# Moving the difference of the split fields from GpSimd to VectorE for ten fields, and loading fields five ahead

## Chip, cores, metric

One core of one Trainium2 chip. The metric is the device time of one execution in microseconds (us), lower is better. The kernel before took 770.79 us in the three runs that came with it (769.37 to 772.43).

## The reference, cut

```python
# inputs: (1024, 32, 128) fp32; W: (496, 128, 128) fp32, one matrix for each pair i < j of the 32 fields
v_i = inputs[:, I_IDX, :]
v_j = inputs[:, J_IDX, :]
transformed = jnp.einsum('bpd,ped->bpe', v_i, W)
return transformed * v_j          # (1024, 496, 128) fp32, 260 MB
```

## The kernel before

Pairs are taken row by row: first the row of field 30 (one pair), then that of 29 (two pairs), down to field 0 (31 pairs). The first 15 pairs use fp32 matmuls as they are ("native"). From pair 15 on, each operand is split into a high part `h`, a low part `l` and a difference `d`, and three faster matmuls take the place of the native one. Splitting a weight chunk (two pairs) is one ScalarE and three GpSimd instructions, splitting a half of a field likewise:

```python
    def split_x(f, a):
        ...
        nc.scalar.mul(h, x_sb[f][:, s], 1.0 - 2.0**-13)
        nc.gpsimd.tensor_tensor(l, x_sb[f][:, s], h.bitcast(F32), ALU.subtract)
        nc.gpsimd.tensor_scalar(l, l.bitcast(F32), 1.0 / EPS, 1.0, ALU.mult, ALU.mult)
        nc.gpsimd.tensor_tensor(d, h.bitcast(F32), l.bitcast(F32), ALU.subtract)
```

A unit is half a pair (512 of 1024 columns). VectorE multiplies each unit's result in PSUM by field j into an output tile of two pairs, of which there are four; a full tile (1 MB) is stored.

```python
    for u in range(2 * NQ + LAG):
        q = u // 2
        if u % (2 * WL) == 0 and (q // WL + WLEAD) * WL < NQ:
            load_w(q // WL + WLEAD)                  # four pairs of weights, 2 KB a partition
        if u < 2 * NQ:
            i, j = pairs[q]
            if u % 2 == 0 and j == i + 1 and 0 <= i - 2 - XLEAD:
                load_x(i - 2 - XLEAD)                # one field, 4 KB a partition
            first(u)                                 # two matmuls, ScalarE scales the sum
        if u >= LAG:
            second(u - LAG)                          # third matmul, VectorE product, store
        ...                                          # every second unit: one split, if any is due
```

All loads but four, and all stores, are issued in order from one queue (SP).

## Time and profile before

| | before |
|---|---|
| time | 770.79 us |
| bytes moved | 310.11 MB: 260.05 MB of results written, 49.28 MB of inputs read, the rest mostly instructions |
| busy: PE, VectorE, ScalarE, GpSimd | 715, 625, 634, 612 us of 769 |
| stretches of 3 us with a DMA share under 0.96, between 3 and 270 us | 6.0 us in sum |

The page's DMA row gives the mean busy share of the 16 DMA engines; in the views of stretches a row has the stretch, its length, the busy time of each engine (with the number of instructions), the granted clock, the DMA share and GB/s. The share can read a little over 1.00 in a full stretch. A stretch whose share is clearly under 1 is called a hole below.

### The profile page before, as it was taken

To read this page: it belongs to the slowest core of one execution; us is meant where nothing else is said; L and a number is where in the kernel's file an instruction comes from. 1 tells how busy PE (TensorE), PEld (TensorE's weight loads), DVE (VectorE), ACT (ScalarE), POOL (GpSimd) and SP (SyncE) were. 2 spreads that over 40 slices of the span, in tenths; PEclk is the share of its full clock that TensorE was granted. 3 is DMA by queue.
4 is the path that set the end of the run, shared out by engine and by line. 5 is a ranking of instruction groups with operands and counts; after the bars stand their busy time and mean duration, and the time that the engine had idled before them with its cause. 6 is when DMAs were issued, how large, how long until landed. Compare 5 with 4: busy or idle time off the path is not lost.

```text
span 769.2 us, 11797 instructions
## 1 busy us (share of the span) xinstructions
PE 715.0 (93%) x2946; PEld 548.9 (71%) x2946; DVE 625.3 (81%) x992; ACT 633.9 (82%) x1256; POOL 611.6 (80%) x883
## 2 busy tenths in 40 slices
PE   7989879889999898999998999999999999999994
PEld 3566657778777686776776877777777777777773
DVE  4767788888988787887787988888888888888885
ACT  2278878888888898898888989898889898998983
POOL 1988998998989878778778697878787869697660
PEclk9999999999999999999999999999999999999997
DMA  9899998999999999999999999999999999999997
GB/s 357 369 411 420 421 400 345 417 410 380 414 422 405 403 395 421 395 416 411 401 420 415 406 414 418 419 415 418 402 419 409 410 410 407 411 413 402 401 399 307
DMA packets 59108, 310.11 MB, mean 403 GB/s; under 512 B 6560, under 2 KB 6816, under 8 KB 27424
## 3 DMA queue, kind: packets, MB, share of 16 engines
q1 hardware_dynamic: 58464, 308.31, 98.8%
q10 hardware_dynamic: 576, 1.05, 0.4%
q8 instruction: 24, 0.39, 0.2%
q14 instruction: 44, 0.36, 0.1%
HBM read 49.28 MB, written 260.05 MB: 402 GB/s over the span
## 4 chain that ended last, share of the span: by engine, by line
PE 49%; DMA 32%; DVE 11%; POOL 6%; issue 1%; DVEq 0%; SPq 0%; ACT 0%; POOLq 0%
DMA out_dram<-ot 31%; PE po L151 31%; PE po L160 15%; DVE ot L166 11%; PE po L148 4%; POOL xd L109 2%; POOL wl L93 1%; POOL xl L107 1%; POOL wd L95 1%; POOL xl L108 0%; DMA x<-in_xt_dram 0%; POOL wd L94 0%; DVEq L166 0%; SPq L74 0%; ACT xh L106 0%
## 5 line engine op out<-in xcount | busy, mean ns | idle before, releaser
L166 DVE TENSOR_TENSOR ot<-po,x 128x512 f32<-128x512 f32 x992 | 625.3, 685 | 135.5 <-DMA out_dram<-ot 71.9
L152 ACT ACTIVATE po<-po 128x512 f32<-128x512 f32 x962 | 549.7, 583 | 109.7 <-PE po L151 61.4
L151 PE MATMUL po<-xh,wh 128*128 128x512 f32 x962 | 387.0, 402 | 25.0 <-DVE ot L166 23.9
L151 PE MATMUL po<-xl,wl 128*128 128x512 f32 x962 | 380.0, 395 | 14.6 <-POOL wl L93 14.1
L160 PE MATMUL po<-xd,wd 128*128 128x512 f32 x962 | 377.3, 393 | 0.0
L151 PEld LDWEIGHTS po<-xh,wh 128*128 128x128 f32 x962 | 181.5, 189 | 96.8 <-DVE ot L166 58.4
L93 POOL TENSOR_TENSOR wl<-w,wh 128x256 fp32r<-128x256 f32 x241 | 177.8, 738 | 74.2 <-ACT wh L92 74.2
L151 PEld LDWEIGHTS po<-xl,wl 128*128 128x128 f32 x962 | 181.9, 189 | 53.9 <-POOL wl L93 19.7
L160 PEld LDWEIGHTS po<-xd,wd 128*128 128x128 f32 x962 | 182.0, 189 | 39.0 <-ACT po L152 0.4
L95 POOL TENSOR_TENSOR wd<-wl,wd 128x256 fp32r<-128x256 f32 x241 | 177.8, 738 | 20.1
L94 POOL TENSOR_SCALAR wd<-wh 128x256 fp32r<-128x256 f32 x241 | 97.4, 404 | 20.3
L92 ACT ACTIVATE wh<-w 128x256 fp32r<-128x256 f32 x241 | 99.0, 412 | 0.0
L107 POOL TENSOR_TENSOR xl<-x,xh 128x512 fp32r<-128x512 f32 x52 | 67.2, 1292 | 17.0 <-ACT xh L106 17.0
L109 POOL TENSOR_TENSOR xd<-xh,xl 128x512 fp32r<-128x512 f32 x52 | 67.0, 1288 | 4.3
L106 ACT ACTIVATE xh<-x 128x512 fp32r<-128x512 f32 x52 | 32.5, 629 | 11.9 <-DMA x<-in_xt_dram 11.7
L108 POOL TENSOR_SCALAR xl<-xl 128x512 fp32r<-128x512 f32 x52 | 32.2, 620 | 4.6
L148 PE MATMUL po<-x,w 128*128 128x512 f32 x60 | 28.9, 647 | 3.9 <-DMA x<-in_xt_dram 3.9
L148 PEld LDWEIGHTS po<-x,w 128*128 128x128 f32 x60 | 12.3, 207 | 19.7 <-issue 15.1
L106 ACT ACT_TABLE_LOAD x1 | 1.3, 1283 | 2.6 <-issue 2.6
L203 POOL MEMSET const-float32-0.0<- 128x1 f32 x1 | 0.1, 98 | 0.2 <-issue 0.2
L203 POOL MEMSET const-bfloat16-1.0<- 128x1 bf16 x1 | 0.1, 101 | 0.0
L203 POOL MEMSET const-uint8-127<- 128x1 uint8 x1 | 0.1, 101 | 0.0
(1 smaller groups left out, 0.1 us busy)
## 6 DMA issues: line engine op xcount, KB each, us to landing
out_dram<-ot SPq DMA_DIRECT2D x247, 1024.0 KB, 8.9
w<-in_wt_dram SPq DMA_DIRECT2D x123, 256.0 KB, 9.1
x<-in_xt_dram SPq DMA_DIRECT2D x30, 512.0 KB, 9.2
x<-in_xt_dram ACTq DMA_DIRECT2D x4, 256.0 KB, 4.9
out_dram<-ot SPq DMA_DIRECT2D x4, 256.0 KB, 7.0
w<-in_wt_dram SPq DMA_DIRECT2D x1, 192.0 KB, 3.5
w<-in_wt_dram SPq DMA_DIRECT2D x1, 64.0 KB, 2.9
```

Source lines behind the costliest of these rows:

```text
L92: nc.scalar.mul(h, raw, 1.0 - 2.0**-13)
L93: nc.gpsimd.tensor_tensor(l, raw, h.bitcast(F32), ALU.subtract)
L94: nc.gpsimd.tensor_scalar(d, h.bitcast(F32), EPS, 1.0, ALU.mult, ALU.mult)
L95: nc.gpsimd.tensor_tensor(d, l.bitcast(F32), d.bitcast(F32), ALU.subtract)
L106: nc.scalar.mul(h, x_sb[f][:, s], 1.0 - 2.0**-13)
L107: nc.gpsimd.tensor_tensor(l, x_sb[f][:, s], h.bitcast(F32), ALU.subtract)
L109: nc.gpsimd.tensor_tensor(d, h.bitcast(F32), l.bitcast(F32), ALU.subtract)
L148: nc.tensor.matmul(po[u], w_raw[q // WL][:, q % WL, :], x_sb[i][:, s], start=True, stop=True)
L151: nc.tensor.matmul(po[u], w_s[c][t][:, r], x_s[i][t][:, s], start=t == 0, stop=t == 1)
L152: nc.scalar.mul(po[u], po[u], 1.0 + EPS)
L160: nc.tensor.matmul(po[u], w_s[q // WC][2][:, r], x_s[i][2][:, s], start=False, stop=True, skip_group_check=True)
L166: nc.vector.tensor_tensor(ots[g][:, k, s], po.pop(u), x_sb[j][:, s], ALU.mult)
```

## The change

The intent: GpSimd, which the early rows wait for, gives up the difference of the ten fields split first (25 to 16), and VectorE forms it, at most ten units after the split was issued; fields are fetched five rows ahead instead of three.

```diff
+SHARED = 10
+XDLAG = 10
-XLEAD = 3
+XLEAD = 5
...
     def split_x(f, a, u):
...
-        nc.gpsimd.tensor_tensor(d, h.bitcast(F32), l.bitcast(F32), ALU.subtract)
+        if f > NF - 2 - NATIVE - SHARED:
+            later.append((min(u + XDLAG, 2 * first_q[f] + LAG - 1), d, h.bitcast(F32), l.bitcast(F32)))
+        else:
+            nc.gpsimd.tensor_tensor(d, h.bitcast(F32), l.bitcast(F32), ALU.subtract)
...
+        while later and later[0][0] <= u:
+            nc.vector.tensor_tensor(*later.pop(0)[1:], ALU.subtract)
```

More of the change, by code (lines that the diff above doesn't have):

```diff
@@ L85, with split_w @@
     w_s = {}
-    def split_w(c):
+    def split_w(c, u):
         k = c * WC % WL
@@ L98, with split_x @@
     x_s = {}
-    def split_x(f, a):
+    later = []
+    def split_x(f, a, u):
         if a == 0:
@@ L118 @@
     for c in range(c0, nchunk):
-        todo.append(((c - 3) * WC + 1, max(c * WC, nq0), lambda c=c: split_w(c)))
+        todo.append(((c - 3) * WC + 1, max(c * WC, nq0), lambda u, c=c: split_w(c, u)))
     for i in range(NF - 2 - NATIVE, -1, -1):
         for a in range(0, BT, HB):
-            todo.append((first_q[i + 1] + 1 if i < NF - 3 - NATIVE else 2, first_q[i], lambda i=i, a=a: split_x(i, a)))
+            todo.append((first_q[i + 1] + 1 if i < NF - 3 - NATIVE else 2, first_q[i], lambda u, i=i, a=a: split_x(i, a, u)))
     todo.sort(key=lambda t: t[1])
@@ L185 @@
             if ready:
-                ready[0][2]()
+                ready[0][2](u)
                 todo.remove(ready[0])
-    assert not todo
+        while later and later[0][0] <= u:
+            nc.vector.tensor_tensor(*later.pop(0)[1:], ALU.subtract)
+    assert not todo and not later
 def kernel(**inputs):
```

## The prediction

> **What bounds the kernel now.** I read the page first (part 1 and the DMA lines), then the busy time by stretches, cut ever finer, then the waits, then the DMA queue's own waits in the first 60 us, last the order of instructions on each engine. The page:
>
> ```profile
> span 769.2 us, 11797 instructions
> PE 715.0 (93%) x2946; PEld 548.9 (71%) x2946; DVE 625.3 (81%) x992; ACT 633.9 (82%) x1256; POOL 611.6 (80%) x883
> DMA  9899998999999999999999999999999999999997
> DMA packets 59108, 310.11 MB, mean 403 GB/s; under 512 B 6560, under 2 KB 6816, under 8 KB 27424
> ```
>
> No compute engine is full, but the DMA row is 9 nearly everywhere: 310.11 MB have to move, the same bytes before and after. So I look for the places where the DMA was not full. Busy time by stretches (columns: PE, PEld, VectorE, ScalarE, GpSimd, then granted clock, DMA share, GB/s):
>
> ```profile
> 3.00:33.00 30.00, 29.09 (x62) 12.77 (x63) 20.02 (x30) 4.12 (x8) 15.63 (x18) 1.00 1.03 416
> 33.00:36.00 3.00, 3.00 (x15) 2.45 (x14) 1.61 (x3) 2.65 (x6) 2.83 (x5) 1.00 0.15 59
> 36.00:114.00 78.00, 68.39 (x279) 52.09 (x277) 59.47 (x94) 63.12 (x128) 70.70 (x96) 0.98 1.01 413
> 117.00:120.00 3.00, 3.00 (x10) 2.36 (x10) 1.94 (x3) 1.41 (x4) 2.75 (x5) 0.66 0.48 191
> 120.00:123.00 3.00, 3.00 (x15) 2.49 (x14) 3.00 (x6) 2.80 (x6) 2.69 (x5) 1.00 0.77 279
> 177.00:180.00 3.00, 3.00 (x14) 2.48 (x13) 2.59 (x5) 2.43 (x5) 2.44 (x4) 0.99 0.77 314
> 180.00:744.00 564.00, 540.90 (x2291) 422.45 (x2290) 473.71 (x762) 498.78 (x987) 456.30 (x669) 1.00 1.01 410
> ```
>
> From 180 to 744 us the DMA share is 1.01 at 410 GB/s: that stretch is DMA-bound and nothing in the change touches its bytes. The holes are early: 33:36 loses 0.85 x 3 = 2.55 us, 117:123 loses 1.56 + 0.69 = 2.25 us, 177:180 loses 0.69 us, together **5.5 us**. A further half microsecond goes at 267:270 (share 0.82), past the changed fields. The start (share 0.32 in the first 3 us: 2 us) and the end (last pairs without loads, last stores landing, about 5 us) stay.
>
> What made the holes? The waits of the whole run, and the DMA queue's waits in 0:60:
>
> ```profile
> POOL wl L93 <- ACT wh L92: 74.2, 99, 2.0
> DVE ot L166 <- DMA out_dram<-ot: 71.9, 84, 3.3
> PEld po L151 <- POOL wl L93: 19.7, 14, 2.7
> PE po L151 <- POOL wl L93: 14.1, 13, 2.3
> ```
>
> ```profile
> SPq L83 <- POOL wl L93: 8.8, 1, 8.8
> ```
>
> VectorE waits 71.9 us for stores to free an output tile: the DMA bound again. PE waits for GpSimd's `wl` 14.1 us; cut by stretches nearly all of it lies before 200 us: 3.1 us in 38:115, 2.3 us (one wait) in 115:135, 5.2 us in 135:173. The wait at 115.7 us stands right before the hole at 117, and in the order of instructions GpSimd there does an x split (1.30 + 0.62 + 1.26 us) ahead of that `wl`. The 8.8 us wait of the DMA queue is one weight load, held until 34.2 us, when GpSimd's third `wl` ends; the stores stand behind it in the same queue, the previous store was issued at 25.0, and the DMA ran dry at 33. So the early holes all carry GpSimd's name.
>
> **What the skill says.** "VectorE: DVE Perf Modes", section on the TRN2 errata, gives (N+151)/0.96 ns for an fp32 `tensor_tensor`, 691 ns at N = 512. The trace has 685 ns for VectorE's 128x512 product and, back to back, 2.50 us for 4, so 0.625 us each: agreed. "SBUF — State Buffer", section "Who interferes with whom", says that a VectorE instruction with two SBUF inputs contends with a GpSimd instruction that reads SBUF, and that whichever comes second fully blocks. Before has no such VectorE instruction (its first input is in PSUM), so this trace can't show it; it does show GpSimd's 128x512 subtraction at 1.27 us at 16 us and 1.30 at 111 us beside a busy VectorE, so today's products don't disturb it. "HBM Reference", section "Specifications (TRN2)", has about 425 GB/s for a core streaming alone; the trace's 410 to 416 over long stretches is close under that, so a faster DMA isn't to be hoped for.
>
> **The change, part by part.** Fields 25 to 16 (ten, two halves each) lose GpSimd's `xd` subtraction: 20 x 1.29 (row L109, 1288 ns) = 25.8 us off GpSimd. VectorE gains 20 x about 0.65 = 13 us, and if the lock holds each also waits up to one GpSimd instruction (0.4 to 1.3 us, mean maybe 0.5), so 13 to 23 us; and GpSimd is stopped 20 x 0.65 = 13 us. Net relief of GpSimd: 13 to 26 us, all before about 200 us.
>
> Against the DMA, row by row. A row with n pairs moves n x (0.524 MB out + 0.066 MB weights) and one field of 0.524 MB, at 413 GB/s: 1.43 n + 1.27 us. GpSimd before, by its cadence (a weight chunk of two pairs starts every 1.98 us, a half field every 3.28 us): 0.99 n + 6.56. First row after the native ones, n = 6: GpSimd 12.5 against DMA 9.9; equal at n = 12. Summed over n = 6 to 12, GpSimd lacks 9.3 us, of which the fields fetched ahead cover a part: that fits 5.5 us of holes. After: two halves cost 2 x 1.99 = 4.0, with the lock 5.3 us; GpSimd then needs 0.99 n + 5.3, at n = 6 11.2 against 9.9, and lacks 2.9 us in all with the lock, 0 without. VectorE after, at n = 6: 12 x 0.625 + 2 x 1.1 = 9.7 against 9.9; at n = 10 14.7 against 15.6. Tight, but under the DMA. PE: 2 x 0.68 n, 8.2 at n = 6.
>
> The start: GpSimd begins at 16.35 us, because ScalarE waits 11.7 us for field 25, and its first four half fields last until 29.5. With five ahead, fields 25 and 24 come in front of three weight loads of 0.26 MB each (0.79 MB, 1.9 us at 416 GB/s), so the split starts about 2 us earlier, and without four subtractions (5.2 us) GpSimd reaches its weight chunks some 7 us sooner. That pays the 2.9 us above, and the held weight load goes out at about 27 instead of 34.2, near where its buffer comes free anyway. The two extra fields (1.05 MB, 2.5 us of DMA) also fill the stage in which the PE's native matmuls limit the stores. They delay weight loads 2 and 3 by 2.5 us; these are needed from pair 8, at about 20 us by the order of the PE's 0.86 us units, so this hides.
>
> Sum: 5.5 us of holes, of which I expect 4.5 to 5 closed: **770.8 - 4.8 = 766.0 us**. The 25.8 us off GpSimd do not appear as such: the DMA needs 310.11 MB at 412 GB/s = 753 us, plus about 2 of start and 5 of end, about 760, whatever the engines do.
>
> **Rivals.** (1) VectorE becomes the bound early: its subtractions stand in its queue ten units after the split was issued; if GpSimd's part is late, or the lock makes each cost over 1.2 us, VectorE stalls behind them, output tiles fill later, and new holes open. For it: VectorE is at 76% in 36:114 and 86% in 123:177, and would reach 95% with the lock. Against: in flight stores give several us of slack, and what it waits for now is mostly the stores. It would make 769 to 773. (2) GpSimd's wait is off the path and the DMA is the bound anyway, so nothing moves: 770. For it: DMA share 1.01 in most of the early stretch too. Against: the holes are real and not filled later, as the rest is full. (3) Everything closes, the hole at 267 too, and the faster early start lets the DMA run nearer 416: 761 to 763. A gain over 2% (under 755.4) would need the DMA to exceed 412 GB/s all along; a loss over 2% (786) needs 16 us of new stalls in 190 us.
>
> **Range and chances.** Predicted 766.0; 8 in 10 between 762 and 770.5. Faster by over 2%: 0.02; within 2%: 0.96; slower: 0.02.
>
> **What would show it.** Right: DMA share above 0.9 in 33:36 and in 114:123; PE's wait for `wl` down from 14 us to a few; the SP queue's single 8.8 us wait gone; first x split at about 14 us; GpSimd's busy time down by about 26 us, `xd` subtractions of VectorE at about 0.65 us; long stretch after 200 us at 410 GB/s, unchanged. If the lock is at work, GpSimd's subtractions or VectorE's lengthen or idle gaps of 0.3 to 1.3 us stand before VectorE's `xd` rows. Wrong: holes of the DMA in new places with VectorE waiting for GpSimd's `xl`, PE waiting for `xd`, or a DMA rate in the full stretches that changes by over 1%, which would move the time by more than all of this.

## More of the kernel before

One more line of the page is wanted later, the chain that ended last:

```profile
PE 49%; DMA 32%; DVE 11%; POOL 6%; issue 1%; DVEq 0%; SPq 0%; ACT 0%; POOLq 0%
```

This chain goes back from the last instruction to what released each step; a third of it is waiting for stores, and 6% is GpSimd.

## The result, and the profile after

The changed kernel took 769.43 us (767.85 to 771.70, six runs) against 770.96 us (769.37 to 772.43, six runs) for the kernel before: ratio 0.9981, 95% interval 0.9960 to 1.0002. Ratios here are the mean time of one kernel's runs over that of the other's of the same rounds, so not quite the ratio of the medians. The gain is some 1.5 us, and the interval just includes none; 4.8 us were forecast. The profiled execution was the slowest of the six (771.70 us).

The page after, its first lines and the DMA row:

```profile
span 769.8 us, 11824 instructions
PE 722.7 (94%) x2946; PEld 545.4 (71%) x2946; DVE 632.0 (82%) x1012; ACT 638.7 (83%) x1256; POOL 593.2 (77%) x863
DMA  9999999999999999999999999999999999999997
```

GpSimd has 20 instructions fewer and is busy 18 us less (by groups, which overlap a little, 26 us less on the difference and some 6 more on the rest, of which below), VectorE has 20 more. The 8 in the second place of the DMA row before and the one in the seventh are gone. The stretches that were holes:

```profile
33.00:36.00 3.00, 3.00 (x15) 2.48 (x14) 1.74 (x4) 2.36 (x6) 0.81 (x2) 1.00 1.00 419
63.00:66.00 3.00, 3.00 (x11) 2.36 (x11) 2.05 (x3) 2.55 (x6) 1.77 (x2) 0.76 0.72 302
117.00:120.00 3.00, 2.84 (x13) 2.02 (x12) 3.00 (x6) 2.38 (x6) 2.75 (x5) 1.00 1.00 414
120.00:123.00 3.00, 3.00 (x15) 2.50 (x14) 2.68 (x5) 3.00 (x7) 2.15 (x4) 1.00 1.04 402
177.00:180.00 3.00, 3.00 (x15) 2.48 (x14) 2.65 (x5) 2.80 (x7) 1.88 (x3) 1.00 1.04 436
180.00:744.00 564.00, 545.27 (x2277) 419.89 (x2276) 470.54 (x759) 499.69 (x981) 453.94 (x666) 1.00 1.01 407
```

All four holes are closed (shares 0.15, 0.48, 0.77, 0.77 before). One new hole of note stands at 63 us, 0.8 us in size. Yet the span did not fall, and the long stretch after 180 us ran at 407 instead of 410 GB/s. The waits:

```profile
DVE ot L172 <- DMA out_dram<-ot: 70.2, 83, 2.1
PE po L166 <- DVE xd L195: 5.7, 4, 2.4
PE po L157 <- POOL wl L95: 2.1, 5, 0.5
```

PE's wait for GpSimd's low part of the weights fell from 14.1 to 2.1 us, as forecast. A new wait of PE for VectorE's difference is 5.7 us, in 4 places; the longest, 2.4 us, ends at 58.9 us, ahead of the new hole. VectorE's wait for stores is as long as before (70.2 against 71.9 us). The chain that ended last, after:

```profile
DMA 61%; DVE 21%; PE 15%; issue 2%; DVEq 0%; SPq 0%; ACT 0%
```

GpSimd has left the chain, and the DMA has taken its place and much of PE's.

**The shared port.** The Trainium skill ("SBUF — State Buffer", "Who interferes with whom") says that a VectorE instruction with two SBUF inputs and a GpSimd instruction that reads SBUF block each other (the lock of the prediction). The trace after shows it. VectorE's difference, by its tile (shortest, median, longest in ns), then GpSimd in order of time around the first three of them, which start at 19.20, 22.03 and 24.54 us (start, length):

```profile
L195 DVE TENSOR_TENSOR xd<-xh,xl x20: 674/690/1711, 19.2 to 173.1; 128x512 fp32r<-128x512 f32 x20
```

```profile
18.39 0.62 POOL L111 TENSOR_SCALAR xl<-xl 128x512 fp32r<-128x512 f32 x1
19.09 1.27 POOL L110 TENSOR_TENSOR xl<-x,xh 128x512 fp32r<-128x512 f32 x1
20.45 0.94 POOL L111 TENSOR_SCALAR xl<-xl 128x512 fp32r<-128x512 f32 x1
...
24.65 0.84 POOL L96 TENSOR_SCALAR wd<-wh 128x256 fp32r<-128x256 f32 x1
```

Undisturbed the difference takes 0.68 us. The first, issued at 19.20 just after a GpSimd subtraction of 1.27 us began, took 1.71 us. GpSimd's scaling took 0.94 instead of 0.62 us next to it, and that of a weight chunk 0.84 instead of 0.40 us next to the third. The mean of the 20 is 831 ns, so VectorE pays 16.6 us for them, within the 13 to 23 us of the prediction.

So in this profile every local step held: relief, holes, waits, lock. What did not follow is the time. The experiments ask why.

### The profile page after: what moved, and what is told of

It is laid out like the page before. It is cut to its first block, busy times and chain, and to the rows that moved or that the text cites. A ratio compares the mean times of both kernels' runs of the same rounds, so it can differ in the third digit from the quotient of the medians.

```text
span 769.8 us, 11824 instructions
## 1 busy us (share of the span) xinstructions
PE 722.7 (94%) x2946; PEld 545.4 (71%) x2946; DVE 632.0 (82%) x1012; ACT 638.7 (83%) x1256; POOL 593.2 (77%) x863
## 2 busy tenths in 40 slices
DMA packets 59108, 310.11 MB, mean 403 GB/s; under 512 B 6560, under 2 KB 6816, under 8 KB 27424
## 4 chain that ended last, share of the span: by engine, by line
DMA 61%; DVE 21%; PE 15%; issue 2%; DVEq 0%; SPq 0%; ACT 0%
DMA out_dram<-ot 60%; DVE ot L172 19%; PE po L157 9%; PE po L166 4%; DVE xd L195 2%; PE po L154 1%; DMA x<-in_xt_dram 1%; DVEq L172 0%; SPq L85 0%; DVEq L217 0%; ACT po L158 0%; DVEq L195 0%
## 5 line engine op out<-in xcount | busy, mean ns | idle before, releaser
L172 DVE TENSOR_TENSOR ot<-po,x 128x512 f32<-128x512 f32 x992 | 618.6, 684 | 129.5 <-DMA out_dram<-ot 70.2
L97 POOL TENSOR_TENSOR wd<-wl,wd 128x256 fp32r<-128x256 f32 x241 | 180.0, 747 | 20.1
L96 POOL TENSOR_SCALAR wd<-wh 128x256 fp32r<-128x256 f32 x241 | 99.1, 411 | 20.3
L115 POOL TENSOR_TENSOR xd<-xh,xl 128x512 fp32r<-128x512 f32 x32 | 41.4, 1292 | 2.7
L154 PEld LDWEIGHTS po<-x,w 128*128 128x128 f32 x60 | 12.1, 206 | 20.2 <-issue 13.9
L195 DVE TENSOR_TENSOR xd<-xh,xl 128x512 fp32r<-128x512 f32 x20 | 16.6, 831 | 0.0
```

The lines of the kernel that those rows point to most:

```text
L96: nc.gpsimd.tensor_scalar(d, h.bitcast(F32), EPS, 1.0, ALU.mult, ALU.mult)
L97: nc.gpsimd.tensor_tensor(d, l.bitcast(F32), d.bitcast(F32), ALU.subtract)
L154: nc.tensor.matmul(po[u], w_raw[q // WL][:, q % WL, :], x_sb[i][:, s], start=True, stop=True)
L172: nc.vector.tensor_tensor(ots[g][:, k, s], po.pop(u), x_sb[j][:, s], ALU.mult)
```

## The experiments

### Is the gain real, and which part closes the holes?

Theory R: the DMA gives back what the holes return. Theory N: the first comparison was unlucky and the gain is near 4.8 us. Four kernels on one chip, five rounds each: the changed kernel again, the kernel before again, and each part of the change alone.

```diff
-XLEAD = 5
+XLEAD = 3        # VectorE's difference alone, in the changed kernel
```

```diff
-XLEAD = 3
+XLEAD = 5        # the earlier loads alone, in the kernel before
```

The changed kernel again: 

> The changed kernel unaltered, for a second profile and a tighter ratio. Theory R (the DMA gives the closed holes back by a lower rate): ratio 0.997 to 0.999, holes of the DMA before 270 us at 2 us or less, and over 270 to 740 us a rate 1 to 2 GB/s below that of the kernel before. Theory N (the first profile was an unlucky run, the gain is really near the 4.8 us predicted): ratio 0.994 to 0.996 and an equal rate in 270 to 740 us.

The kernel before again: 

> The kernel before against itself: ratio 1.000 within 0.0015, which says how small a difference can be seen. Its profile should again show DMA holes of 5 to 6.5 us before 270 us after the first 3 us, if they belong to the schedule and not to one run; theory R wants its rate in 270 to 740 us at about 411 GB/s again.

VectorE's difference alone: 

> VectorE forms the difference, fields three ahead as before. If the hole at 33 us came from GpSimd alone, it is closed here too (DMA share over 0.9). If it needed the two extra fields, it stays (2 us or more). Theory R: time 769 to 771 whichever; theory N: 766 to 768, most of the gain being in this part.

Earlier loads alone: 

> Fields five ahead, GpSimd forms the difference as before. The hole at 33 us should shrink, those at 117 and 177 us stay, as GpSimd lacks the same 9 us in the rows of 6 to 12 pairs. Theory R: 769.5 to 771; theory N: 768 to 769.5 (about 2.5 us of the gain). A rival, that the early loads cost by standing before weights, would give 771 to 773.

| kernel | median us | ratio to before | 95% interval |
|---|---|---|---|
| changed, again | 767.26 (765.67 to 776.66) | 0.9975 | 0.9933 to 1.0017 |
| before, again | 772.88 (769.73 to 774.61) | 1.0019 | 0.9994 to 1.0043 |
| difference on VectorE alone | 767.15 (766.14 to 771.75) | 0.9956 | 0.9927 to 0.9984 |
| five ahead alone | 769.88 (766.64 to 773.72) | 0.9985 | 0.9952 to 1.0017 |

A kernel against itself gave 1.0019, so 0.2% cannot be told from nothing here, and the parts cannot be ranked. The changed kernel's interval holds both R's 0.997 to 0.999 and N's 0.994 to 0.996 (the medians of this chip, 771.15 for before, are 3.9 us apart, and one run of 776.66 us pulls the mean up); only the first comparison, 0.9960 to 1.0002, speaks against 4.8 us, which would be 0.9938. Of the stretches that were holes, those shown are first of the kernel before again, then with the difference on VectorE alone, then with the earlier loads alone:

```profile
33.00:36.00 3.00, 3.00 (x14) 2.43 (x13) 1.83 (x3) 2.26 (x5) 2.66 (x6) 1.00 0.20 85
117.00:120.00 3.00, 3.00 (x10) 2.33 (x10) 2.00 (x3) 1.47 (x4) 2.75 (x5) 0.67 0.96 351
120.00:123.00 3.00, 3.00 (x15) 2.47 (x14) 2.99 (x6) 2.80 (x6) 2.73 (x5) 1.00 0.81 329
177.00:180.00 3.00, 3.00 (x15) 2.46 (x14) 2.36 (x4) 2.80 (x6) 2.83 (x5) 1.00 0.96 393
```

```profile
33.00:36.00 3.00, 3.00 (x15) 2.46 (x14) 1.89 (x4) 3.00 (x7) 1.54 (x3) 1.00 1.04 426
```

```profile
33.00:36.00 3.00, 2.99 (x14) 2.10 (x12) 1.47 (x3) 2.96 (x7) 2.55 (x6) 1.00 1.00 412
117.00:120.00 3.00, 2.60 (x11) 2.17 (x12) 1.83 (x3) 1.75 (x3) 2.67 (x6) 1.00 1.02 426
120.00:123.00 3.00, 3.00 (x15) 2.46 (x15) 3.00 (x6) 2.79 (x6) 2.83 (x5) 1.00 0.93 366
177.00:180.00 3.00, 3.00 (x15) 2.49 (x14) 3.00 (x5) 2.80 (x7) 2.83 (x5) 1.00 1.02 410
```

The hole at 33 us comes again in the kernel before and is closed with either part. That at 120 us comes again as well (share 0.81, 0.77 in the first profile), but those at 117 and 177 us are all but gone (0.96 each instead of 0.48 and 0.77), with nothing changed. I had expected 5 to 6.5 us of holes again; by the count that gave 6.0 us it was 3.6. So the full shares with the earlier loads alone at 117 and 177 us, where I had expected the holes to stay, do not show that these loads closed them. In the run with these loads alone the holes were only 0.9 us between 3 and 270 us, and the profiled execution took 771.7 us. Closed holes and a time that can't be told from before thus go together without VectorE's work, too. Theory R's second half, a lower rate because holes were closed, is not borne out as a rule: in stretches without holes between 36 and 741 us the rate was 410.7 and 409.1 GB/s in the two profiles of before, 407.4 and 409.9 in those of after. It varies from run to run by as much as it would have to differ.

### Does VectorE's new work eat the gain?

Nobody forms the difference for the ten fields; the third matmul reads the low part (wrong; the comparison still passed it as correct, so its tolerance does not see that small term). Fields three ahead.

```diff
-            later.append((min(u + XDLAG, 2 * first_q[f] + LAG - 1), d, h.bitcast(F32), l.bitcast(F32)))
+            x_s[f][2] = x_s[f][1]
```

> Fields three ahead; for the ten fields nobody forms the difference, and the third matmul reads the low part instead (wrong on purpose): GpSimd's relief without VectorE's work. If VectorE's work, its waits for GpSimd or the shared port ate the missing gain, this takes 764 to 766 us against 767 of the run with that work. If the DMA limits either way, it is within 1 us of that run, 766.5 to 769.

It took 769.78 us, above both of my ranges, ratio 0.9972 (0.9948 to 0.9996), with 0.3 us of holes before 270 us. The run with VectorE's work had the ratio 0.9956, on another chip. So the difference, its lock and its waits cost nothing that can be seen: the ratios' intervals leave them up to some 1.6 us, half of the missing 3.3. As the account of the whole loss, that rival falls.

### What does the DMA take by itself?

Every load and store in the order of the changed kernel, nothing computed; the stores come from four tiles set to zero once. Then the same without weights, without fields, or without both (but for the first four loads of each), and with the layout of either load changed. All give wrong results.

```diff
-            first(u)
         if u >= LAG:
-            second(u - LAG)
+            ... nc.sync.dma_start(out=out[g], in_=fixed[g % 4])   # at the end of each tile
```

All loads and stores: 

> All loads and stores of the changed kernel in their order, nothing computed, stores out of four tiles that are set to zero once (the result is wrong on purpose). Nothing but the DMA can limit it. If the DMA's own limit is what holds the kernels in their full stretches, it runs at 407 to 413 GB/s and takes 752 to 762 us. If the kernels' rate is lowered by their engines or by how the stores come, it runs at 418 GB/s or more and takes under 748 us.

Stores alone: 

> The same without the loads of weights and of most fields (260.05 MB of stores and some 3 MB of loads, wrong on purpose). If reads and writes cost the DMA alike, the rate is the same as with loads and the time is 0.85 of it, some 645 us at 408 GB/s; if the stores are the slower part, the rate is under 403 GB/s and the time above 650 us.

Without weights: 

> The DMA alone (nothing computed, wrong on purpose) without 120 of the 124 weight loads, 31.5 MB. If a byte costs the same in either direction at the 416 GB/s of the stores alone, the time falls by 76 us from 771 to 695. If the weight loads in 2 KB rows are the slow part, it falls by 95 us or more.

Without fields: 

> The DMA alone without 28 of the 32 fields, 14.7 MB. At 416 GB/s the time falls by 35 us to 736. If the field loads, whose rows of 4 KB lie 128 KB apart in memory, are the slow part, it falls by 50 us or more; the dips of the rate to 300 to 390 GB/s after each field load speak for that.

Weights in 4 KB rows: 

> The DMA alone with weights in 4 KB rows (eight pairs a load instead of four), the same bytes. If the 2 KB rows cost, 755 to 763 us; if not, 771 as with four.

Fields in one piece: 

> The DMA alone with each field lying in one piece in memory (rows of 4 KB one behind the other), the same bytes. If the distance between rows costs, 755 to 765 us and no dips after field loads; if not, 771.

| the DMA alone | median us | before on the same chip |
|---|---|---|
| all loads and stores | 771.05 (766.99 to 774.51) | 771.82 |
| stores alone | 633.39 (633.36 to 633.42) | 771.82 |
| without weights | 678.27 (676.55 to 679.80) | 770.52 |
| without fields | 708.84 (708.36 to 717.95) | 770.52 |
| weights in 4 KB rows | 757.90 (756.35 to 758.53) | 770.52 |
| fields in one piece | 770.40 (767.44 to 774.23) | 770.52 |

**This is the first half of the answer.** With no engine to wait for and no hole at all, the DMA takes 771 us, the time of the kernel before (ratio 0.9984, 0.9954 to 1.0013). That is not the least it can take: the same bytes take 758 us with weights in 4 KB rows and 756 us with stops (below). I had worked out 760 us as the least from 412 GB/s, the rate of the kernel's own full stretches. The rate is no constant. The DMA alone, all loads and stores, in three stretches (columns: stretch, length, VectorE, GpSimd, clock, DMA share, GB/s):

```profile
36.00:180.00 144.00, 0.00 (x0) 0.00 (x0) 1.00 1.02 424
180.00:380.00 200.00, 0.00 (x0) 0.00 (x0) 1.00 1.01 413
396.00:740.00 344.00, 0.00 (x0) 0.00 (x0) 1.00 1.01 401
```

The share is full throughout, but the rate falls from 424 GB/s early, with many fields among the stores and weights, to 401 late, with few or none. Stores alone keep 420 to the end and repeat within 0.06 us; with reads the time spreads over 7 us. On top of the stores, the 14.7 MB of fields cost 45 us (678 less 633) and the 31.5 MB of weights 75 us (709 less 633), both together 138, which is 17 us more than the sum (the runs without one of them were on another chip). By the byte, the weights alone cost what the stores cost (31.5 MB in 75 us is 417 GB/s); the fields cost more (327 GB/s), and so does having both. The distance between the rows of a field does not matter (770.4).

### Does a hole cost its length?

The Trainium skill ("DMA: Bandwidth & Descriptors", "Why a DMA increments its semaphore by 16 and not by 1") explains that the up to 16 engines of one transfer finish independently, each signals for itself, and only all 16 mean that the data has landed. The trace has these 16 landings of each transfer. The spread from the first to the last, worked out from these records, median over stretches of 60 us:

```
us from          60   180   300   420   540   660
before          4.7   3.8   4.4   4.4   4.9   4.6
changed         4.0   4.8   4.8   4.8   4.7   4.8
DMA alone       0.3   7.0  10.6  10.4  10.9  11.0
stores alone    0.6   0.5   0.7   0.9   0.9   (ends at 631)
```

In the DMA alone after 200 us, 14 engines land within 0.8 us of each other, the 15th 5 us and the 16th 10.7 us behind the first. In the kernels, where only four output tiles are in flight, the last is 4.6 us behind the first. The same skill page, section "Latency and other measured facts", says that engines 7 and 15 are usually slower than the rest; its guess at a cause is crowded ports where GpSimd's DMA path keeps its descriptors, and it says that this belongs to that path alone. Here two lag as well, but nearly all of these transfers are issued from SP, and stores alone show no lag, so that guess does not cover this lag. Which two they are, the trace does not tell.

So a hole in the mean share may leave the last engine busy. The hole of before at 117 to 123 us is such a one. The six transfers landing before it and the one after it (us; first, median of the 16, 15th, last):

```
first   median  15th    last
111.9   112.4   113.8   115.9
112.6   113.1   114.4   116.5
115.1   115.6   116.9   119.0
117.5   118.0   119.5   121.8
118.1   118.6   120.1   122.5
124.4   124.7   125.0   125.2
```

The next store was issued at 120.1 us. From about 119 us most engines had nothing to do, but the last worked until 122.5, when its piece of the next store already waited. The hole let the others stand until it had caught up: the spread fell from 4.3 to 0.8 us. By the records of packets, the time in which no engine at all had a packet in flight, between 4 and 740 us, is **1.4 us** in the kernel before (all of it in the hole at 33 us), of 6.0 us of holes counted by the mean share; in its second profile and in both of the changed kernel it is 0.0.

Two experiments make holes on purpose. In the changed kernel, VectorE does 40 needless products in the middle:

```diff
+        if u == STALL:                      # 560
+            for _ in range(NSTALL):         # 40
+                nc.vector.tensor_tensor(scratch, x_sb[31][:, 0:256], x_sb[30][:, 0:256], ALU.mult)
```

> The changed kernel, and in the middle (before unit 560) VectorE does 40 needless products of 256 columns into a scratch tile, some 14 us, so that the stores dry up. The hole in the DMA should be 5 to 12 us. If a hole costs its length, the time rises by that length over the changed kernel's 767 to 769. If the DMA runs faster after a hole and gives part of it back, the rate in the 100 us after it is above that before it, and the time rises by clearly less than the hole.

In the DMA alone, four stores wait until VectorE has rewritten their tile three times, once the last store from it has landed in all pieces:

```diff
+                if g in (120, 150, 180, 210):
+                    for _ in range(NST):    # 3
+                        nc.vector.tensor_tensor(fixed[g % 4] ..., ALU.mult)   # in place
```

> The DMA alone, with four stops in the second half: there one store waits for VectorE to rewrite its tile three times, some 7 us, after the last store from it has landed in all 16 pieces (wrong on purpose). The mean busy share should show 15 us or more of holes in all. If a hole costs its length, the time rises by that, to 785 us or more. If the lagging engine sets the pace and works through the stops, the time stays at 767 to 773 us, and the spread between the first and the last piece falls after each stop and grows again.

The kernel with the long stop took 787.63 us, 15.8 us over before on that chip (ratio 1.0195, 1.0171 to 1.0219). If the changed kernel, which was not run there, is 0.2% below before there too, the stop cost some 17 us; against its medians on other chips it is 18 to 20. The stop and the stretches around it:

```profile
330.00:446.00 116.00, 110.66 (x464) 86.48 (x464) 97.08 (x156) 100.97 (x201) 91.74 (x135) 0.99 1.01 407
447.00:468.00 21.00, 0.24 (x2) 0.00 (x0) 19.73 (x38) 0.81 (x2) 7.24 (x9) 0.62 0.16 67
530.00:740.00 210.00, 204.47 (x881) 163.50 (x880) 183.14 (x292) 189.55 (x377) 168.41 (x251) 1.00 1.01 411
```

Stretches of 3 us count 20.0 us of hole, the time with no packet in flight is 16.6 us: which of the two the cost follows, this run cannot tell. A hole that stops every engine is paid nearly in full.

The DMA alone with stops took 755.87 us (754.39 to 758.67), ratio 0.9801 (0.9776 to 0.9827): **with stops it is 15 us faster than without**. Before, in and after the first stop:

```profile
180.00:380.00 200.00, 0.00 (x0) 0.00 (x0) 1.00 1.01 414
...
381.00:384.00 3.00, 0.56 (x1) 0.00 (x0) 1.00 0.20 85
384.00:387.00 3.00, 2.97 (x2) 0.00 (x0) 1.00 0.06 27
387.00:390.00 3.00, 2.97 (x2) 0.00 (x0) 1.00 0.06 25
396.00:740.00 344.00, 20.63 (x9) 0.00 (x0) 1.00 1.01 420
```

The stop shows 9.0 us of hole in the mean share and 0.0 us without a packet in flight. It brought the spread from 10.2 to 0.2 us, and it stayed under 1 us to the end; the rate from 396 to 740 us was 420 GB/s, where the run without stops had 401. The other three stops found no lag to wait for and no hole shows at them. I had expected an unchanged time at best. Here 9 us of hole in the mean share came with a shorter time, so the mean share is no safe measure of lost time. That the lag itself lowers the rate is not shown, though: the DMA alone without weights (spread 13.9 us) and with weights in 4 KB rows (12.0 us) lagged more and moved 421 and 417 GB/s from 396 to 600 us, where the run with everything moved 402. The stop raised the later rate; whether by ending the lag or by shifting the transfers against each other, no run separates.

### Can a lower bound of the DMA be used?

Weights in 4 KB rows made the DMA alone 13 us faster. Both kernels with these rows (three load buffers of double size; one buffer fewer for `wh` to make room), and the changed one with fields in pairs as well:

```diff
-WL = 4
+WL = 8
-WLEAD = 4
+WLEAD = 2
```

```diff
+            if u % 2 == 0 and j == i + 1 and i % 2 == 0 and 0 <= i - 3 - XLEAD:
+                load_x(i - 3 - XLEAD, 2)     # the third kernel only
```

Before with 4 KB rows: 

> The kernel before with weights in 4 KB rows (eight pairs a load, three buffers of double size, one buffer less for the high part of the split weights), otherwise unaltered. The DMA alone took 758 us so. If the DMA's own time bounds the kernel, it falls to 758 to 764 us; if GpSimd's relief is what matters, it stays near 769 or more.

Changed with 4 KB rows: 

> The changed kernel with weights in 4 KB rows. If the DMA bounds both, 757 to 762 us, and 2 to 5 us under the kernel before with these rows, as less lag hides the early holes less.

Changed with 4 KB rows and fields in pairs: 

> The same and fields loaded in pairs, 8 KB a row. Taking the fields away from the DMA alone saved 62 us for 14.7 MB, so if their 4 KB rows are part of that, this is 3 us or more below the run with weights in 4 KB rows alone (753 to 758); if not, equal to it within 1.5 us.

They took 775.85, 770.25 and 771.98 us, ratios 1.0052 (1.0020 to 1.0084), 0.9986 (0.9959 to 1.0012) and 1.0001 (0.9978 to 1.0024). None came below 764, as I had expected if the DMA's own time bounds them; the kernel before met the other branch (769 or more, if GpSimd's relief is what matters), and the third missed its 753 to 758 and lies 1.7 us above the second. The time of the DMA alone, 758 us, is therefore not a bound that a kernel reaches by the same change of rows, and its agreement with the kernels at 2 KB rows, 771 us, may in part be chance: the DMA alone has a lag of 10 us and the kernel one of 4.6 us, so the two need not lose the same rate (argued, not shown). With these rows the change is worth more, 5.6 us between the medians of one chip, with intervals that do not overlap. The holes of before are larger again (share 0.41 at 117 us): 4.5 us by the mean share, 1.1 us in the changed kernel with these rows, while the time without a packet in flight is 0.0 in both. So here the count of holes comes nearer to the gain than that of packets in flight. The edit also alters how far weights are fetched ahead and takes a buffer away; I have not separated the causes.

### Do the spread loads of fields keep the lag up?

The last two kernels load all fields, or those up to twelve ahead, at the start, after the first weights.

```diff
-XLEAD = 5
+XLEAD = 28       # and 12
```

All at the start: 

> The changed kernel with every field loaded at the start, after the first weights. The early stores stand behind 14 MB of loads (some 35 us), but the DMA stays busy. If the spread loads of fields keep the engines apart, the spread of the 16 pieces falls under 2 us after 100 us, the rate rises to 415 GB/s or more and the time falls to 750 to 760 us. If not, the spread is 4 to 5 us as before and the time 768 to 775 us.

Twelve ahead: 

> The changed kernel with fields twelve ahead. Between the two: if the spread loads matter, the last field load comes at about 330 us instead of 440 and the time falls by 2 to 5 us; if not, within 1.5 us of the changed kernel (767 to 770).

They took 767.04 us (767.01 to 767.85) and 768.46 us (766.06 to 769.15), ratios 0.9919 (0.9889 to 0.9949) and 0.9931 (0.9897 to 0.9966). By the ratios both would be 0.5 to 0.6% below the changed kernel (0.9981, 0.9960 to 1.0002), and the first one's interval lies outside of that. But before took longer on this chip than on any other (773.47), and against the changed kernel's times on others (767.3 and 769.4) little or nothing is left; the changed kernel was not run here, so a gain stays open. The first lines of the waits with all fields at the start:

```profile
DVE ot L174 <- DMA out_dram<-ot: 59.2, 53, 27.6
...
PE po L156 <- DVE ot L174: 23.6, 1, 23.6
```

One wait of 23.6 us holds PE at the start, and the kernel is not slower for it: the DMA had work meanwhile. The spread was 1.4 to 2.1 us from 60 to 300 us, but it grew back to 4.4 us at 360 us, long after the last field had landed. So in the kernel the lag returns without field loads.

## Why the prediction was right or wrong

- **The DMA is the bound: right.** Taking every engine out leaves 771 us; a wait of PE of 23.6 us cost nothing.
- **Which holes, and that they close: right.** All four closed, PE's wait for GpSimd fell to 2.1 us, the DMA queue's wait of 8.8 us is gone, the first split began at 14.25 us. One new hole of 0.8 us stands right behind PE's waits for VectorE's difference at 59 and 61 us, as rival 1 has it; the second profile of the changed kernel does not have it. But those at 117 and 177 us were all but gone in the second profile of before, too, so for these two luck has a part in it.
- **"So the early holes all carry GpSimd's name": not shown.** With earlier loads alone, and all of GpSimd's subtractions, the stretches were full as well, and I had given these loads only the start. Nor does "nearly all" of PE's wait for `wl` lie before 200 us: 10.6 of 14.1 us lie before 173 us and 3.4 behind 192 us.
- **The cost on VectorE: right.** 16.6 us, with the lock at work; leaving the work out changed nothing that could be seen. Of the working, the 0.625 us for a product back to back does not agree with the 691 ns of the page, as I wrote; the 685 ns of one product does, and so does an undisturbed difference, 0.68 us.
- **"Sum: 5.5 us of holes, of which I expect 4.5 to 5 closed": this step failed.** I took the dips of the mean share of 16 DMA engines in one profile for lost time that the schedule costs in every run. What the runs showed: the second profile of before has 3.6 us by the count that gave 6.0; by the packets in flight, only 1.4 us of the first profile (0.0 of the second) was time in which no engine worked, and in the rest at least one went on, in the hole at 117 us the one that lags by 4.3 us; and the profiles without these holes came with a gain of only 1.5 us (0 to 3). That 1.5 is near 1.4 may be chance: with weights in 4 KB rows some 5 us were gained where no such time stood. Which part of a dip is lost stays open.
- **"The DMA needs 310.11 MB at 412 GB/s = 753 us": failed too.** The rate is not given: the same stores and loads ran at 401 or at 420 GB/s from 396 to 740 us, without and with a stop before. I also gave the rival "the DMA is the bound anyway, so nothing moves" too little weight against the holes being real.
- The range, 762 to 770.5 us, held the measured 769.43 us; its centre was 3.4 us too low. That the time fell into the range says little: before itself, 770.96 us, lies only 0.5 us above it.

What stays open: what a closed hole is worth, what makes one or two engines lag when there are reads, whether the lag costs anything, why the lag returns in the kernel within 60 us of a stop (spread 1.8 us from 480 us, 4.2 us from 540 us) but not in the DMA alone, and whether a kernel can be had that keeps it away. No run of a whole kernel here is clearly faster than the changed kernel.

## What to carry to other kernels

When the DMA is full nearly everywhere, do not book a dip of its mean share as time to be won: profile the same kernel twice and see whether the dip comes again, and ask whether all of the 16 engines stand still in it. Run the transfers alone before tuning engines; where that takes as long as the kernel, work on the transfers, and take neither that time for a floor nor the rate of the full stretches for a constant. With a forecast gain under 1%, run the kernel against itself first: here that alone gave 0.2%.

## What the Trainium skill lacked or had wrong

- "DMA: Bandwidth & Descriptors": it does not say by how much single engines lag, or whether that costs rate. Here the last lands 4.6 us behind the first in the kernels and 10.7 us in the DMA alone. After a stop that brought the spread from 10.2 to 0.2 us the rate was 420 instead of 401 GB/s; but other mixes of transfers lagged by 12 and 14 us at 417 and 421 GB/s.
- The same page, on slower engines: its guess, about descriptors of GpSimd's path, leaves a lag of 5 and 10.7 us in transfers issued from SP without a cause, with none over 1 us when there are stores alone.
- No page says what reads among the stores cost: on top of 633 us for the stores, weights took 75 us for 31.5 MB, the rate of the stores, but fields 45 us for 14.7 MB, and 17 us more went when both were there.
